# Moving one group's statistics, a few evictions and the first head sums in the prologue of a gated cross-attention block

## The chip, the cores and the metric

One core of one Trainium2 chip. The metric is the device time of one execution in microseconds (us). Times inside a profile count from the start of its span. All arithmetic is float32.

## The reference, cut to what matters

```python
x = x + tanh(g_xattn) * attention(layernorm(x), ctx)   # 16 heads of 64, softmax over 77 keys, then Wo and bo
x = x + tanh(g_ffn) * (layernorm(x) @ W[idx] + b[idx])  # idx: the arg max of logits + gumbel noise
```

x is (4, 2048, 512), the context (4, 77, 384). The layernorms divide by the standard deviation of each row.

## The kernel before, in words

The 8192 rows of x are cut into 16 groups of 512 rows, four groups per batch entry. Weights are folded first: Wq and the keys become one matrix `m` per batch entry (scores = x @ m), the values and Wo become `vo` (attention output = p @ vo), and the chosen W, centred and scaled by its gate, becomes `wf`. So each group needs three products: scores, attend, and the feed-forward one.

Each product is a `Seven`: a block multiplication done with seven half-size products instead of eight. `product(s)`, for s = 0 to 6, issues the matmuls of one of the seven on TensorE (L461). `post(s)` takes its PSUM bank out: for three or four of the seven it is a copy by ScalarE (L467), for the others an addition by VectorE (L486). Two of the three banks of a `Seven` are read and then added to further: product 2 adds to the bank that `post(0)` has read, product 4 to the one that `post(2)` has read, product 6 to the one that `post(4)` has read. So a late `post` stops TensorE. The extra operands (T1 to T4) are sums made by GpSimd (L432), those of the weights likewise (L123).

The order of the work is written out by hand, and each engine takes its instructions in that order. A PSUM pool has seven banks for matmul results. The change lies in the prologue, which TensorE passes between 53 and 150 us:

1. `s0`, `s1`, `s2` for group 0: scores in three `Seven`s. Between their steps stand the layernorm statistics of groups 0 and 1, and the weights `wf`: `centre_wf` (a matmul with ones at L637, four VectorE subtractions at L639) and `scale_wf` (eight ScalarE activations at L644).
2. `s0` for group 1, and between its steps the last of eight `build_vo(p, engines)`: six matmuls each (L331), six evictions with the gate's scale, by VectorE (L334) or ScalarE (L336) as the letters of `engines` say in turn, and four stores to DRAM by SyncE's queue. Beside it runs the softmax of group 0: `head_max` (L524, L526), 64 exponentials on ScalarE (L532, each 128x77), `head_sum` (L539 and a reciprocal, L540) and `head_scale` (GpSimd, L543).
3. `s1` and `s2` for group 1 together, twelve matmul records a step. Between their steps `p_columns` transposes the softmax result of group 0 on VectorE (L552; each transpose reads all four heads).

Then the loop over groups 1 to 15 starts with `at` for group 0 (tile `ps_a`), then the feed-forward product (`ps_f`) with the first scores of a later group laid between.

The statistics of a group (class `Norms`) have four steps: `stats` (16 VectorE BN statistics, L365), `gather` (eight ScalarE copies, L374), `calc` with `power` (seven small VectorE operations, L381 to L388, and a power on GpSimd, L393), and `back` (four ScalarE copies, L398, then `down` and `up` on GpSimd, L403 and L404). `norm_step(n, 0)` is `gather`, `norm_step(n, 1)` is `calc` and `power`, `norm_step(n, 2)` is `back`. Group 1's `down` and `up` are first read by its `head_max` and exponentials, in the loop.

Of the kernel before, what the change touches and what calls it, by code (L numbers as in the profile page):

```python
# [19 lines left out]
def flamingo_block_kernel(  # L20
# [34 lines left out]
    NT, D = x.shape  # L55
# [32 lines left out]
    def bank(name):  # L88
        return pm.tile([P, 512], F32, tag="mm", name=name)
# [29 lines left out]
    def weight_sum(w, n, engine=None):  # L119

        to, a, b_, op = ((5, 0, 3, ALU.subtract), (3, 3, 2, ALU.add), (4, 3, 0, ALU.subtract),
                         (6, 1, 4, ALU.subtract))[n]
        (engine or nc.gpsimd).tensor_tensor(flat(w[:, to]), flat(w[:, a]), flat(w[:, b_]), op)  # L123
# [23 lines left out]
    xg, ys, ts_ = {}, {}, {}  # L147
# [4 lines left out]
    def load(i):  # L152
        xg[i] = row_tile("xg")
        for a in range(NA):
            nc.sync.dma_start(out=xg[i][ts(a, 32)], in_=rows_of(x, i)[:, :, ts(a, P)])
# [33 lines left out]
    def by_chunk(t):  # L189

        return t.rearrange("p (a q e) -> p q a e", a=NA, e=32)

    def chunked(t):
        return t.rearrange("p (q a e) -> p q a e", a=NA, e=32)
# [127 lines left out]
    def build_vo(p, engines):  # L322
        n = 0
        for c in range(3):
            r = min(P, BP - c * P)
            for hh in range(2):
                stg = vo_st[(2 * p + hh) % len(vo_st)]
                hr = ts(hh, DH)
                v = vT[p][hr].rearrange("p r b k -> p (r b k)")
                ps = bank("ps_vo")  # L330
                nc.tensor.matmul(ps[:r, :], v[:, ds(c * P, r)], wo[hr, p, :], start=True, stop=True)  # L331
                src, dst = by_chunk(ps[:r, :]), chunked(stg[:r, c, :])
                if engines[n % len(engines)] == "D":
                    nc.vector.tensor_scalar(dst, src, tgx[:r], None, ALU.mult)  # L334
                else:
                    nc.scalar.activation(dst, src, AF.Copy, scale=tgx[:r])  # L336
                n += 1
        for hh in range(2):
            d, stg = vo_d[2 * p + hh], vo_st[(2 * p + hh) % len(vo_st)]
            nc.sync.dma_start(out=d[0 : 2 * P].rearrange("(c r) e -> r c e", r=P), in_=stg[:, 0:2])  # L340
            nc.sync.dma_start(out=d[2 * P :], in_=stg[: BP - 2 * P, 2])
# [5 lines left out]
    def load_vo(bi):  # L347
        src = vo_d.rearrange("h (r b k) e -> (h r) b k e", b=B, k=NK)[:, bi]
        for o, c in ((0, 0), (1, 0), (1, 1), (0, 1)):
            nc.sync.dma_start(out=vo[:, BLK[o, c]], in_=src[:, ts(c, KH), ts(o, D // 2)])  # L350
# [161 lines left out]
    def s_rows(i, k, cols):  # L512
        if i not in sc:
            sc[i] = wp.tile([P, HA, NG, JP], F32, tag="s", name="s")
        nc.vector.transpose(key_chunk(sc[i], k), cols.rearrange("p (g h r) -> p g h r", h=HA, r=R))  # L515

    def head(i, h):
        return sc[i][:, h, :, :J]
# [3 lines left out]
    def head_max(i, h):  # L522
        mx = stat[:, ds((16 + h) * NG, NG)]
        nc.vector.tensor_reduce(mx, head(i, h), AX.X, ALU.max)  # L524
        nmx[h] = small.tile([P, NG], F32, tag=f"nmx{h}", name="nmx")
        nc.vector.tensor_tensor(nmx[h], mx, norms[i].down, ALU.mult)  # L526

    def exps(i, n0, n1):

        for n in range(n0, n1):  # L530
            h, g = n // NG, n % NG
            nc.scalar.activation(head(i, h)[:, g, :], head(i, h)[:, g, :], AF.Exp,  # L532
                                 scale=norms[i].up[:, g : g + 1], bias=nmx[h][:, g : g + 1])
# [3 lines left out]
    def head_sum(i, h):  # L537
        sums[h] = sm = small.tile([P, NG], F32, tag=f"sm{h}", name="sm")
        nc.vector.tensor_reduce(sm, head(i, h), AX.X, ALU.add)  # L539
        nc.vector.reciprocal(sm, sm)  # L540

    def head_scale(i, h):
        nc.gpsimd.tensor_tensor(head(i, h), head(i, h), sums[h].unsqueeze(2).to_broadcast([P, NG, J]),  # L543
                                ALU.mult)

    def p_columns(i, k0, k1):
        for k in range(k0, k1):
            if k == 0:
                t = wp.tile([P, NK * T + KH * T2], F32, tag="pT", name="pT")
                pT[i] = Columns(t[:, : NK * T].rearrange("p (n t) -> p n t", t=T),  # L550
                                T1=t[:, NK * T :].rearrange("p (n t) -> p n t", t=T2))
            nc.vector.transpose(pT[i].all[:, k, :].rearrange("p (g h r) -> p g h r", h=HA, r=R),  # L552
                                key_chunk(sc[i], k))
# [75 lines left out]
    def sum_wf(wfr):  # L629
        t = wf_f[:, :D]  # L630
        nc.gpsimd.tensor_tensor(t, wfr[:, 0, :], wfr[:, 1, :], ALU.add)
        nc.gpsimd.tensor_tensor(t, t, wfr[:, 2, :], ALU.add)
        nc.gpsimd.tensor_tensor(t, t, wfr[:, 3, :], ALU.add)

    def centre_wf(wfr):
        ps = bank("ps_w")
        nc.tensor.matmul(ps, ones, wf_f[:, :D], start=True, stop=True)  # L637
        for c in range(NDC):
            nc.vector.tensor_tensor(wfr[:, c, :], wfr[:, c, :], ps, ALU.subtract)  # L639

    def scale_wf(wfr):
        for c in range(NDC):
            for o in range(2):
                nc.scalar.activation(chunked(wf[:, BLK[o, c // 2], c % 2, :]),  # L644
                                     by_chunk(wfr[:, c, :])[:, ts(o, 2)], AF.Copy, scale=tgf)
# [10 lines left out]
    def norm_step(n, s):  # L656
        if s == 0:
            n.gather()
        elif s == 1:
            n.calc()  # L660
            n.power()
        elif s == 2:
            n.back()
# [20 lines left out]
    for s in range(7):  # L684
        s1.product(s)
        if s == 0:
            s1.post(0)
            s0.product(6)
            s0.post(6)
            norm_step(n, 0)  # L690
            for k in range(2):
                s_rows(0, KH + k, s0.chunk(1, k))
            sum_wf(wfr)
        elif s == 1:
            norm_step(n, 1)
        elif s < 4:
            n1.stats(xg[1], 0, 8 * (s - 2), 8)
        if 0 < s:
            s1.post(s)
        if s == 3:  # L700
            norm_step(n, 2)
            norm_step(n1, 0)
        if s == 4:
            centre_wf(wfr)
        if s == 5:
            scale_wf(wfr)
            for k in range(2):
                s_rows(0, 2 + k, s1.chunk(0, k))
# [3 lines left out]
    for s in range(7):  # L712
        s2.product(s)
        s2.post(s)
        if s == 0:
            norm_step(n1, 1)
        if s == 3:
            norm_step(n1, 2)
        if s == 5:
            s_rows(0, 4, s2.chunk(0, 0))  # L720
            load(2)
# [14 lines left out]
    for s in range(6):  # L736
        s0.product(s)
        s0.post(s)
        if s < 4:
            build_vo(4 + s, "D" if s == 2 else "DDA")  # L740
        if s < 2:
            head_max(0, 2 + s)
        exps(0, e[s], e[s + 1])
        if s == 3:
            load_vo(0)
        if s in (2, 4, 5):
            h = (None, None, 0, None, 1, 2)[s]
            head_sum(0, h)
            head_scale(0, h)
    for s in range(7):  # L750
        s1.product(s)
        s2.product(s)
        if s == 0:
            s1.post(0)
            s2.post(0)
            exps(0, 57, 64)
            s0.product(6)
            s0.post(6)
            weight_sum(wf, 0)
            head_sum(0, 3)  # L760
            head_scale(0, 3)
        if 1 <= s < 5:
            p_columns(0, (0, 2, 5, 7)[s - 1], (2, 5, 7, 10)[s - 1])
        if s == 2:
            pT[0].sum("T1")
        if s == 3:
            weight_sum(vo, 0)
        if s == 4:
            weight_sum(vo, 1)
        if s == 5:  # L770
            weight_sum(vo, 2)
            for k in range(4):
                s_rows(1, (0, 1, KH, KH + 1)[k], s0.chunk(k // 2, k % 2))
        if 0 < s:
            s1.post(s)
            s2.post(s)
# [161 lines left out]
    n1, n0 = Norms(NGRP + 1, NG // 2), Norms(NGRP + 2, NG // 2)  # L938
# [144 lines left out]
```

## Time and profile before

| | |
|---|---|
| three timed runs | 1263.45, 1261.90, 1262.99 us; median 1262.99 |
| the profiled execution | 1262.86 us, its span 1261.1 us |
| busy: TensorE matmul, weight load | 1241.8 us, 1060.5 us |
| busy: VectorE, ScalarE, GpSimd | 915.6, 686.3, 876.8 us |
| mean granted TensorE clock | 0.996 |

The span runs from the first to the last instruction; 1.8 us of the execution lie around it. "Busy" is the sum of an engine's instructions. A bracket behind an instruction in a timeline is the time that its engine stood idle before it, and the arrow names what ended that. PEclk is the clock that TensorE was granted, 1.00 being full speed. A name such as `snap L467` is the tile that an instruction writes and its line in the kernel.

### The profile page before, as it was taken

To read this page: it belongs to the slowest core of one execution; us is meant where nothing else is said; L and a number is where in the kernel's file an instruction comes from. 1 tells how busy PE (TensorE), PEld (TensorE's weight loads), DVE (VectorE), ACT (ScalarE), POOL (GpSimd) and SP (SyncE) were. 2 spreads that over 40 slices of the span, in tenths; PEclk is the share of its full clock that TensorE was granted. 3 is DMA by queue.
4 is the path that set the end of the run, shared out by engine and by line. 5 is a ranking of instruction groups with operands and counts; after the bars stand their busy time and mean duration, and the time that the engine had idled before them with its cause. 6 is when DMAs were issued, how large, how long until landed. Compare 5 with 4: busy or idle time off the path is not lost.

```text
span 1261.1 us, 16981 instructions
## 1 busy us (share of the span) xinstructions
PE 1241.8 (98%) x5704; PEld 1060.5 (84%) x5704; DVE 915.6 (73%) x1857; ACT 686.3 (54%) x1966; POOL 876.8 (70%) x470
## 2 busy tenths in 40 slices
PE   9999899999999999999999999999999999999996
PEld 6565788888888888888888888888888888888885
DVE  5788766777776767777776777666777876666577
ACT  3447473827456483736548373654738274564823
POOL 4343796685968778584968778575986877585766
PEclk9999999999999999999999999999999999999999
DMA  9776400304106030303306030122304111010102
GB/s 267 275 219 209 117 1 1 68 21 110 20 1 151 1 67 1 66 2 90 62 1 151 1 67 1 24 44 84 67 1 109 43 42 26 1 34 1 34 1 67
DMA packets 95221, 80.27 MB, mean 64 GB/s; under 512 B 3856, under 2 KB 83088, under 8 KB 95136
## 3 DMA queue, kind: packets, MB, share of 16 engines
q1 hardware_dynamic: 92768, 76.74, 24.1%
q10 hardware_dynamic: 1760, 1.34, 0.3%
q8 instruction: 45, 0.74, 0.3%
q0 software_dynamic: 608, 1.13, 0.2%
q14 instruction: 40, 0.33, 0.1%
HBM read 44.07 MB, written 35.13 MB: 63 GB/s over the span
## 4 chain that ended last, share of the span: by engine, by line
PE 94%; DVE 3%; ACT 2%; POOL 0%; issue 0%; DVEq 0%; POOLq 0%; ACTq 0%
PE ps_a L461 38%; PE ps_s L461 36%; PE ps_f L461 15%; PE ps_kv L266 2%; PE ps_vo L331 1%; PE ps_m L296 1%; ACT s L532 1%; DVE pT L552 0%; PE ps_w L167 0%; DVE vo L334 0%; DVE snap L486 0%; ACT wf L644 0%; ACT snap L467 0%; DVE t L412 0%; DVE z L219 0%
## 5 line engine op out<-in xcount | busy, mean ns | idle before, releaser
L461 PE MATMUL ps_a<-pT,vo 128*128 128x256 f32 x2240 | 486.2, 379 | 0.0
L461 PEld LDWEIGHTS ps_a<-pT,vo 128*128 128x128 f32 x2240 | 425.6, 190 | 57.9
L532 ACT ACTIVATE s<-s,nmx,up 128x77 f32<-128x77 f32 x1024 | 355.8, 444 | 0.0
L432 POOL TENSOR_TENSOR pT<-pT 128x1280 f32<-128x1280 f32 x64 | 185.8, 2904 | 173.2 <-PE ps_a L461 163.7
L461 PE MATMUL ps_s<-tq,m 128*128 128x256 f32 x1280 | 293.0, 381 | 6.0 <-DVE sn L486 3.3
L461 PEld LDWEIGHTS ps_s<-tq,m 128*128 128x128 f32 x1280 | 243.4, 191 | 44.1 <-DVE sn L486 3.7
L467 ACT COPY snap<-ps_s 128x512 f32<-128x512 f32 (+1 forms) x188 | 93.5, 515 | 283.5 <-DVE t L412 131.3
L461 PE MATMUL ps_s<-xc,m 128*128 128x256 f32 x960 | 221.4, 380 | 0.0
L461 PEld LDWEIGHTS ps_s<-xc,m 128*128 128x128 f32 x960 | 182.0, 190 | 29.0 <-DVE vo L334 2.4
L543 POOL TENSOR_TENSOR s<-s,sm 128x1232 f32<-128x1232 f32 x64 | 145.2, 2269 | 65.2 <-DVE sm L540 50.2
L486 DVE TENSOR_TENSOR snap<-snap,ps_s 128x512 f32<-128x512 f32 (+1 forms) x141 | 83.4, 593 | 122.7 <-PE ps_s L461 118.6
L461 PE MATMUL ps_f<-tq,wf 128*128 128x256 f32 x512 | 118.4, 379 | 0.4 <-DVE snap L486 0.4
L552 DVE STREAM_TRANSPOSE pT<-s 128x512 f32<-128x512 f32 x160 | 101.0, 677 | 15.9 <-POOL s L543 15.9
L393 POOL TENSOR_TENSOR r<-r,neghalf 32x16 f32<-32x16 f32 (+1 forms) x33 | 93.1, 2832 | 25.8 <-DVE r L388 25.2
L539 DVE TENSOR_REDUCE sm<-s 128x16 f32<-128x1232 f32 x64 | 91.5, 1430 | 25.8 <-ACT s L532 25.8
L432 POOL TENSOR_TENSOR tq<-xc,tq 128x512 f32<-128x512 f32 x64 | 85.3, 1332 | 34.8 <-PE ps_f L461 32.3
L461 PEld LDWEIGHTS ps_f<-tq,wf 128*128 128x128 f32 x512 | 97.2, 190 | 13.9 <-issue 0.7
L515 DVE STREAM_TRANSPOSE s<-snap 128x512 f32<-128x512 f32 x156 | 99.8, 685 | 8.6 <-ACT snap L467 6.4
L524 DVE TENSOR_REDUCE ps_st<-s 128x16 f32<-128x1232 f32 x64 | 92.4, 1444 | 2.1
L432 POOL TENSOR_TENSOR tq<-xc 128x512 f32<-128x512 f32 x64 | 81.6, 1274 | 14.4 <-DVE xc L407 13.1
L461 PE MATMUL ps_f<-xc,wf 128*128 128x256 f32 x384 | 90.7, 379 | 0.0
L467 ACT COPY snap<-ps_f 128x512 f32<-128x512 f32 x63 | 36.9, 586 | 89.1 <-PE ps_f L461 89.1
(126 smaller groups left out, 1183.6 us busy)
## 6 DMA issues: line engine op xcount, KB each, us to landing
xg<-in_x_dram SPq DMA_DIRECT2D x64, 256.0 KB, 6.0
out_dram<-y SPq DMA_DIRECT2D x60, 256.0 KB, 4.5
vo<-vo_d SPq DMA_DIRECT2D x16, 640.0 KB, 6.7
vo_d<-vo SPq DMA_DIRECT2D x16, 512.0 KB, 4.2
m<-m_d SPq DMA_DIRECT2D x12, 640.0 KB, 4.2
m_d<-vo SPq DMA_DIRECT2D x4, 960.0 KB, 7.5
wq<-in_WqT_dram SPq DMA_DIRECT2D x8, 256.0 KB, 6.3
wq<-in_Wo_dram SPq DMA_DIRECT2D x1, 2048.0 KB, 13.8
```

The source lines that it names most:

```text
L266: nc.tensor.matmul(ps[:, :n], w[:, c, ts(p, P)], keys[:, c].rearrange("p b j -> p (b j)"), start=(c == 0), stop=(c == NCC - 1))
L393: nc.gpsimd.tensor_tensor(r, r, neghalf[:32, : r.shape[1]], ALU.pow)
L432: (engine or nc.gpsimd).tensor_tensor(self.at[name], self.at[a], self.at[b_], op)
L461: nc.tensor.matmul(self.ps[r][:, n, :], self.w(blk, c, pair), self.cols(cname, c), start=(first and n == 0 and c == 0), stop=(c == h - 1), ...
L467: nc.scalar.copy(dst, self.ps[r])
L486: nc.vector.tensor_tensor(c, c, self.ps[r], ALU.add)
L515: nc.vector.transpose(key_chunk(sc[i], k), cols.rearrange("p (g h r) -> p g h r", h=HA, r=R))
L524: nc.vector.tensor_reduce(mx, head(i, h), AX.X, ALU.max)
L532: nc.scalar.activation(head(i, h)[:, g, :], head(i, h)[:, g, :], AF.Exp, scale=norms[i].up[:, g : g + 1], bias=nmx[h][:, g : g + 1])
L539: nc.vector.tensor_reduce(sm, head(i, h), AX.X, ALU.add)
L543: nc.gpsimd.tensor_tensor(head(i, h), head(i, h), sums[h].unsqueeze(2).to_broadcast([P, NG, J]), ALU.mult)
L552: nc.vector.transpose(pT[i].all[:, k, :].rearrange("p (g h r) -> p g h r", h=HA, r=R), key_chunk(sc[i], k))
```

## The change

In words, in the order of the program:

- Group 1's 16 BN statistics stand in four lots of four, in steps 2 to 5 of group 0's `s1` and each behind that step's `post`, instead of two lots of eight ahead of the `post`s of steps 2 and 3. Its `gather` stands in step 5 (ahead of `scale_wf`) instead of step 3.
- Its `calc` and `power` stand in step 2 of `s2` instead of step 0, its `back` in step 3 of the later loop of group 1's `s1` and `s2`, instead of step 3 of group 0's `s2`.
- Of `build_vo(7)`, two of the six evictions (one of 128x512, one of 64x512) go from ScalarE to VectorE. `build_vo(6)` was by VectorE alone before as well.
- Head sums and scales 0, 1, 2 of group 0 stand in steps 3, 4, 5 of group 1's `s0` instead of steps 2, 4, 5.
- The last seven exponentials stand ahead of the loop of `s1` and `s2`, so ahead of the copies of its first step.

```diff
@@ group 0, s1
         elif s == 1:
             norm_step(n, 1)
-        elif s < 4:
-            n1.stats(xg[1], 0, 8 * (s - 2), 8)
         if 0 < s:
             s1.post(s)
+        if 2 <= s < 6:
+            n1.stats(xg[1], 0, 4 * (s - 2), 4)
         if s == 3:
             norm_step(n, 2)
+        if s == 5:
             norm_step(n1, 0)
         if s == 4:
             centre_wf(wfr)
@@ group 0, s2
         s2.post(s)
-        if s == 0:
+        if s == 2:
             norm_step(n1, 1)
-        if s == 3:
-            norm_step(n1, 2)
@@ group 1, s0
         if s < 4:
-            build_vo(4 + s, "D" if s == 2 else "DDA")
+            build_vo(4 + s, "DDA" if s < 2 else "D")
...
-        if s in (2, 4, 5):
-            h = (None, None, 0, None, 1, 2)[s]
-            head_sum(0, h)
-            head_scale(0, h)
+        if 3 <= s:
+            head_sum(0, s - 3)
+            head_scale(0, s - 3)
+    exps(0, 57, 64)
@@ group 1, s1 and s2
             s1.post(0)
             s2.post(0)
-            exps(0, 57, 64)
             s0.product(6)
...
+        if s == 3:
+            norm_step(n1, 2)
```

No instruction is added or removed; those named change their place, and two change their engine.

## The prediction

> **What bounds the kernel now.** I read the page's busy times first, then TensorE's waits in the prologue, the granted clock around the longest of them, and the chain that ended last.
>
> ```profile
> PE 1241.8 (98%) x5704; PEld 1060.5 (84%) x5704; DVE 915.6 (73%) x1857; ACT 686.3 (54%) x1966; POOL 876.8 (70%) x470
> ```
>
> TensorE is busy 98% of the span, and from 149.81 us to the last groups it shows no idle time. An edit in the prologue is therefore worth what it changes in TensorE's stops before that. These are the stops between 50 and 152 us (in all, times, longest):
>
> ```profile
> PE ps_s L461 <- DVE sn L486: 3.3, 1, 3.3
> PE ps_s L461 <- ACT snap L467: 1.8, 2, 1.5
> PE ps_s L461 <- DVE vo L334: 0.8, 1, 0.8
> PE ps_vo L331 <- DVE snap L486: 0.5, 1, 0.5
> ```
>
> The longest has a tail, which the busy time and granted clock of two stretches show (PEclk is the third figure from the end):
>
> ```profile
> 142.00:145.40 3.40, 0.12 (x1) 0.00 (x0) 3.40 (x8) 0.00 (x0) 3.40 (x2) 1.00 0.01 2
> 145.40:149.80 4.40, 4.37 (x12) 3.53 (x13) 4.40 (x9) 0.59 (x1) 4.26 (x2) 0.61 0.00 0
> ```
>
> Behind the stop the clock averages 0.61, and the twelve matmul records of product 6 take 4.54 us where the twelve before took 2.75. So this stop, E, costs 3.31 + 1.79 = 5.1 us. The 1.46 us stop at 91.69, called B, left the clock at 1.00.
>
> What makes E: the chain that ended last runs there
>
> ```profile
> 131.22 2.42 ACT s L532 x7
> 133.63 0.02 issue
> 133.66 1.45 DVE sm L539
> 135.10 0.02 issue
> 135.13 0.26 DVE sm L540
> 135.39 0.02 issue
> 135.42 0.02 POOLq L543
> 135.43 0.09 issue
> 135.53 2.28 POOL s L543
> 137.80 0.02 issue
> 137.82 0.91 DVE pT L552 x2
> ```
>
> The last exponentials, the last sum and the last scale come ahead of every transpose; post(4), which frees product 6, stands behind ten transposes. What makes B is on ScalarE, here with VectorE's row for the statistics:
>
> ```profile
> 82.09 3.18 DVE L365 BATCH_NORM_STATS2 s<-xg 128x6 f32<-128x128 f32 x16
> ...
> 87.59 3.30 ACT L644 ACTIVATE wf<-wfr,tg 128x256 f32<-128x256 f32 x8
> ...
> 90.80 1.10 ACT L467 COPY snap<-ps_s 128x512 f32<-128x512 f32 x3
> ...
> 91.69 1.13 PE L461 MATMUL ps_s<-tq,m 128*128 128x256 f32 x4 [1.46 <-ACT snap L467]
> ```
>
> TensorE waits for the second of three copies behind scale_wf. Ahead of scale_wf stand the eight gather copies, 85.97 to 87.58.
>
> **Part 1: statistics and gather.** The 16 statistics cost the same 3.18 us, but the last four now stand behind post(3), post(4) (1.25 together), the four subtractions of centre_wf (2.46) and post(5) (0.67). From 82.09 VectorE was busy without a gap until 89.44, and it does the same work in another order: the matmuls that it needs end at 82.17, 83.89, 84.75 and 86.48, each in time. So the last statistic ends at 89.5 instead of 85.27. post(4) is 1.5 us earlier; that lets product 6 of s1 start at 86.32 instead of 86.50, which only lengthens a stop that follows anyway.
>
> gather needs the last statistic, so ScalarE waits from 86.1 to 89.5, and behind the waiting copy are queued gather's other seven (1.61 in all, to 91.1), scale_wf (3.30, to 94.45) and the copies that TensorE waits for. The second of these let TensorE go 0.80 behind scale_wf's end. TensorE resumes at 95.26: B grows by 3.57, from 1.46 to 5.0 us.
>
> Is the clock reduced there? The rows show 1.46 us without and 3.31 us with a reduction. 5.0 lies beyond the second, so I take a reduction, at E's price of 1.79 us. The bounds: 0, and 3.6, twice E's, if the spell is twice as long.
>
> The Trainium skill, "TensorE: Matmul & The Clock Gate" (section "What's actually happening"), says that a free-running window of 3413 ns in which TensorE idles halves its clock. Read strictly, 5.0 us hold a whole window in (5.0 - 3.41) / 3.41 = 47% of the positions; as an estimate that prices the reduction at 0.47 x 1.7 = 0.8 us and the sum below at -1.4. The trace disagrees in part: 3.31 us, less than a window, were enough.
>
> **Part 2: calc and back.** calc stays behind the transposes that wait for s1's last copy, as in the trace (92.63, behind a transpose that waited for ScalarE); it goes along with the 3.57. back leaves a bad place: ScalarE waited 4.32 us for the power and did four copies (0.84) ahead of s2's post(6), which ended at 98.78. Without them post(6) follows product 6 at once: with TensorE 3.57 later it ends at 100.35, only 1.6 later, and group 0's first maximum with it. In its new place back takes 0.85 on ScalarE, inside an idle stretch of 13.50 us; if that cover were gone it would cost 0.85. Its down and up (0.48) stand on GpSimd between T1 and the sums of vo, and that counts below.
>
> **Part 3: evictions, sums, exponentials.** From here all times are at full clock. TensorE starts build_vo(3) at 96.30 + 3.57 = 99.87. It took 24.83 to product 4 of s0 (121.13). In that lie the stops of 0.82 and 0.55, and bank waits inside build_vo(5) (3.20 instead of 2.92) and build_vo(7) (4.18 less 0.55, instead of 3.0). VectorE is now less behind TensorE, so the freed banks come in time: 24.83 - 0.82 - 0.55 - 0.28 - 0.63 = 22.55, product 4 at 122.4.
>
> VectorE: a first eviction follows its matmuls' start by 1.16 (69.73 to 70.89). build_vo(6) starts at 114.5, so its six evictions run from 115.6 for 4.03, to 119.7; post(3) to 120.3; build_vo(7) starts at 119.4, its six evictions run from 120.6 to 124.6. Two of them are new here (0.68 each). Then head_sum 0, 1.42 + 0.25 with gaps, to 126.3; it was at 118.88.
>
> ScalarE: exponentials 24 to 31 end at about 119.9 and nothing stands between them and the rest. In the trace 4.64 us lay between (117.19 to 121.83: two evictions of 0.69 and 0.68, two waits of 1.77 and 1.59, gaps). The other 32 take 32 x 0.346 = 11.1, so the last ends at 131.0 instead of 133.66. That is 2.7 earlier, but late next is GpSimd: scale 0 starts at 126.45, each scale takes 2.27 and a gap, and wf's sum (1.27) stands ahead of the fourth. 126.45 + 4 x 2.28 + 1.27 = 136.85, against 137.80.
>
> From the first transpose to TensorE's restart were 7.61 us (137.82 to 145.43): now 136.87 to 144.5. TensorE arrives at 122.4 + 20.99 = 143.4, the same work as from 121.13 to 142.12. E is 1.1 us, less than B's 1.46, which left the clock alone. Product 6 takes 2.6, and ps_a starts at 147.1 instead of 149.81: -2.7.
>
> **Part 4: what GpSimd gives back.** From 154.37 GpSimd works without a gap past the feed-forward's first sum, and that sum is just in time:
>
> ```profile
> 154.37 5.78 POOL L432 TENSOR_TENSOR pT<-pT 128x1280 f32<-128x1280 f32 x2 [1.64 <-PE ps_a L461]
> ...
> 180.25 1.27 POOL L432 TENSOR_TENSOR tq<-xc 128x512 f32<-128x512 f32 x1
> ```
>
> It ends at 181.52, and TensorE takes it at 181.75. In the changed kernel T1 follows the transposes by 3.17 (140.04), takes 2.91, then down and up 0.48, then three sums of vo 8.87: 152.3. TensorE's first attend product ended before that (151.4). So this run starts 2.07 earlier, not 2.7, and the feed-forward sum ends at 179.45, where TensorE would be at 179.05. The gain shrinks to 2.07 plus the slack of 0.2, about 2.2 us.
>
> The vo stores on SyncE's queue follow the last eviction, 2.6 us later than before, and vo's loads follow these. They landed within 10.6 us of issue; issued from about 128.9 they are in by 141.5, before the sums need them at 143.4. No cost; if they were later, GpSimd would wait one for one.
>
> **Sum.** -2.2 at full clock, +1.79 for the reduction behind B, which shifts all later steps alike: -0.4. The profiled execution took 1262.86, so **1262.5 us**. The runs' median, 1262.99, lies 0.13 above it.
>
> **Rivals.**
> 1. The clock stays full behind B: -2.2, 1260.7 us. For it: no row has a stop of 5 us. Against it: 3.31 sufficed. 16%.
> 2. The spell behind B lasts twice as long: +3.6 instead of +1.8, 1264.3 us. For it: it rests on one spell only. 12%.
> 3. Slower: E stays long as well and its clock reduction comes back. The place is the row of twelve VectorE evictions, head sum 0 and four GpSimd scales. If they end 2.3 us later than summed, E is over 3.3 again, and the total is -0.4 + 2.3 + 1.8 = +3.7: 1266.6 us. For it: head sum 0 stands 7.4 us later than in the trace, behind all evictions; one eviction by itself lasts 0.74, and they waited 0.67 at 113.22. Against it: 12 x 0.07 + 0.67 makes 1.5, not 2.3. 14%.
> 4. gather isn't held up, and B stays 1.46: another 3.57 and no reduction, 1257.1 us. Against it: the copy is ahead of scale_wf in ScalarE's order, and needs the last statistic. 5%.
> 5. The edit does not reach E: the gain at E and the loss at B cancel, 1262.9 us. 5%.
>
> The forecast has the remaining 48%.
>
> **The numbers.** 0.2%, about 2.5 us, is what a measurement of this kernel can tell from no change. Faster by more (under 1260.5): rival 4, a good third of rival 1 (its time lies 0.2 above the bound, and my sums are good to about 0.8), and 6% from the forecast's edge: 17%. Slower by more (over 1265.5): most of rival 3 (13%) and 2% of rival 2: 15%. Within: 68%. The range leaves out rival 4 and rival 3's larger part and holds the clock's bounds (0 to 3.6) with 0.8 of error: 1259.9 to 1265.4.
>
> **What would show it.** Right: the first L374 copy of group 1 idles about 3.4 us for VectorE's L365; TensorE stops some 5 us for snap L467 near 95, with PEclk below 1 behind it; E is near 1 us with PEclk 1.00 behind it; the four scales run nearly back to back; TensorE waits briefly for tq L432 near 180. Wrong: a B under 3 us, an E over 3, or a new stop after 150 us of more than 1.

## The result, and the profile after

| | before | changed |
|---|---|---|
| median of 12 runs each | 1263.40 us | 1262.35 us |
| lowest, highest | 1261.90, 1263.85 | 1260.29, 1263.31 |
| profiled execution, its span | 1262.86, 1261.1 | 1261.98, 1260.2 |

The ratio is 0.9994, with a 95% interval of 0.9986 to 1.0002: no difference that these runs can tell. Beneath it two large ones cancel. These are TensorE's waits between 50 and 200 us in the changed kernel (in all, times, longest), to be read against the four lines of before:

```profile
PE ps_s L461 <- ACT snap L467: 5.6, 2, 5.3
PE ps_s L461 <- DVE sn L486: 0.8, 1, 0.8
PE ps_f L461 <- POOL tq L432: 0.3, 1, 0.3
```

E has shrunk from 3.3 to 0.8 us, and the stops of 0.8 and 0.5 us at the evictions are gone. B has grown from 1.5 to 5.3 us. A new short stop waits for GpSimd's feed-forward sum. How B came about, in the timeline of ScalarE and TensorE (start, duration, in brackets the idle time before):

```profile
89.07 0.19 ACT L374 COPY ps_st<-s 32x32 f32<-32x32 f32 x1 [3.46 <-DVE s L365]
...
90.69 3.30 ACT L644 ACTIVATE wf<-wfr,tg 128x256 f32<-128x256 f32 x8
93.90 1.10 ACT L467 COPY snap<-ps_s 128x512 f32<-128x512 f32 x3
...
94.78 2.07 PE L461 MATMUL ps_s<-tq,m 128*128 128x256 f32 x4 [5.30 <-ACT snap L467]
```

The first gather copy idles 3.46 us for the last statistics. The same eight activations of 3.30 us and the same copies follow, and TensorE goes on after the second of these. The four matmul records there take 2.07 us; before, they took 1.13. The clock tells why (stretches; the first figure behind the length is TensorE's busy time, the third from the end the granted clock):

```profile
88.80:92.10 3.30, 0.68 (x4) 0.25 (x2) 1.39 (x3) 2.93 (x12) 0.00 (x0) 1.00 0.00 0
92.20:95.50 3.30, 0.72 (x2) 0.63 (x3) 1.01 (x2) 2.79 (x8) 0.00 (x0) 0.50 0.00 0
95.60:98.90 3.30, 3.30 (x9) 2.58 (x9) 2.07 (x9) 0.37 (x1) 1.21 (x1) 0.50 0.00 0
99.00:102.00 3.00, 3.00 (x15) 2.13 (x16) 1.78 (x5) 0.37 (x1) 2.92 (x3) 1.00 0.00 0
```

The clock is halved from 92.16 to 98.99 in the trace's clock record, 2.6 us of it inside the stop and 4.2 behind it. From the restart to build_vo(3) TensorE takes 6.57 us (94.78 to 101.35) instead of 4.61 (91.69 to 96.30): the reduction costs 1.96 us.

E, in the timeline of GpSimd, VectorE and TensorE:

```profile
127.85 6.72 POOL L543 TENSOR_TENSOR s<-s,sm 128x1232 f32<-128x1232 f32 x3 [22.20 <-issue]
134.52 1.26 POOL L123 TENSOR_TENSOR wf<-wf 128x512 f32<-128x512 f32 x1
135.75 2.27 POOL L543 TENSOR_TENSOR s<-s,sm 128x1232 f32<-128x1232 f32 x1
...
138.05 4.27 DVE L552 STREAM_TRANSPOSE pT<-s 128x512 f32<-128x512 f32 x7 [4.17 <-POOL s L543]
...
145.65 2.86 PE L461 MATMUL ps_s<-tq,m 128*128 128x256 f32 x12 [0.81 <-DVE sn L486]
```

The last exponentials end at 132.1 and the last reciprocal at 133.9, but GpSimd works through the row of scales without a gap until 138.0. In the profile before, GpSimd stood idle for 2.73 us ahead of the last scale, waiting for the last sum and so for the last exponentials; now its own row of scales sets when the transposes start. The twelve records behind E take 2.86 us, where they took 4.54.

One reading to be careful with: the chain that ended last names a DMA of `xg` (135.38 to 144.08) as what released `down` at 144.08. `down` reads nothing of `xg`; it stands behind T1 on GpSimd, which ran from 141.21 to 144.1. The two ends coincide.

### The profile page after: what moved, and what is told of

Its sections match the earlier page's. It is cut to its first block, busy times and chain, and to the rows that moved or that the text cites. A ratio compares the mean times of both kernels' runs of the same rounds, so it can differ in the third digit from the quotient of the medians.

```text
span 1260.2 us, 16984 instructions
## 1 busy us (share of the span) xinstructions
PE 1241.3 (99%) x5704; PEld 1061.0 (84%) x5704; DVE 914.0 (73%) x1859; ACT 685.6 (54%) x1964; POOL 876.8 (70%) x470
## 3 DMA queue, kind: packets, MB, share of 16 engines
q0 software_dynamic: 608, 1.13, 0.4%
## 4 chain that ended last, share of the span: by engine, by line
PE 93%; POOL 3%; DVE 2%; ACT 1%; DMA 1%; issue 0%; SPq 0%; POOLq 0%; DVEq 0%; ACTq 0%
PE ps_s L461 36%; PE ps_a L461 36%; PE ps_f L461 15%; PE ps_kv L266 2%; PE ps_vo L331 2%; PE ps_m L296 2%; POOL vo L123 1%; DMA xg<-in_x_dram 1%; POOL pT L432 1%; PE ps_w L167 0%; POOL s L543 0%; DVE snap L486 0%; POOL xc L558 0%; ACT wf L644 0%; POOL wf L123 0%
```

## Experiments

The theory was that of the prediction. B: gather's wait delays scale_wf, the copies and TensorE, and the longer stop halves the clock. E: the row of evictions, exponentials, sums, scales and transposes is shorter, until GpSimd bounds it. The ratios are to the kernel before, run on the same chip.

**e1: gather moved behind the copies**

```diff
@@ changed kernel, group 0's s1
-        if s == 5:
-            norm_step(n1, 0)
@@ s2, behind post(s)
+        if s == 1:
+            norm_step(n1, 0)
         if s == 2:
             norm_step(n1, 1)
```

> The changed kernel with group 1's gather moved behind post(1) of s2, so that scale_wf is not behind the last statistic. Theory (the gather's wait is what makes stop B long, and the reduced clock follows from it): TensorE's wait for snap L467 near 90 falls from 5.3 to under 1.5 us, the granted clock there stays 1.00, and the run is 4.5 + 1.9 = 6.4 us faster than the changed kernel, near 1256. Rival (the statistics laid between the posts hold VectorE up, whatever gather does): B stays near 5 and the time near 1262. Rival (everything before E is absorbed at E by something that does not move, such as the loads of vo): B falls, E grows by as much, time near 1262.

Measured: 1256.13 us, ratio 0.9948 (0.9934 to 0.9962) to before. TensorE's waits:

```profile
PE ps_s L461 <- ACT snap L467: 0.8, 2, 0.5
PE ps_s L461 <- DVE sn L486: 0.8, 1, 0.8
```

The statistics are as spread as in the change. The clock stays full, B is down to 0.5, and E is the same 0.8. So the price in the changed kernel was that of gather's place alone, about 6 us (ratios 0.9994 and 0.9948), and nothing later absorbs it.

**e2: statistics and gather as before, the rest as changed**

```diff
@@ changed kernel, group 0's s1
+        elif s < 4:
+            n1.stats(xg[1], 0, 8 * (s - 2), 8)
         if 0 < s:
             s1.post(s)
-        if 2 <= s < 6:
-            n1.stats(xg[1], 0, 4 * (s - 2), 4)
         if s == 3:
             norm_step(n, 2)
-        if s == 5:
             norm_step(n1, 0)
```

> The changed kernel with the statistics and the gather of group 1 where they stood before the change; evictions, head sums, exponentials and the late return stay. Theory: B is back at 1.5 us and full clock, E stays near 0.8, time near 1262.35 - 3.6 - 1.9 = 1257. Rival (the spread statistics are part of what shortens E): E returns to 3 us and its reduced clock, time near 1263.

Measured: 1257.07 us, 0.9954 (0.994 to 0.9967). B is 1.47 us at full clock and E 0.81:

```profile
PE ps_s L461 <- ACT snap L467: 1.8, 2, 1.5
PE ps_s L461 <- DVE sn L486: 0.8, 1, 0.8
```

The spread of the statistics has no part in E's gain; the rest of the change is worth 5.7 us by itself (1262.78 to 1257.07).

**e3: the statistics and the gather alone.** The edit of e2 turned round, made in the kernel before.

> The kernel before with only the statistics and the gather moved as in the change. Theory: B grows to 5 us with a reduced clock behind it and E stays at 3.3 us with its own, so the time is that of before plus 3.6 + 1.8 = 5.4 us, near 1268.8. Rival (a longer B is absorbed in E): at most 2 us slower, near 1265.

Measured: 1267.10 us, 1.0035 (1.0022 to 1.0049): 4.4 us slower (2.8 to 6.2), an interval that holds the 5.4 expected, with the median a microsecond below it. B is 5.30, E 3.31, and the clock falls behind both. The profile shows the missing microsecond: from build_vo(3) to the end of E TensorE takes 48.02 us (102.19 to 150.21) instead of 49.13 (96.30 to 145.43), mostly because the 0.82 us stop of before is not there any more. My expectation had left that out. The reduction behind B costs 1.55 us here: from the restart to build_vo(3) are 6.16 us (96.03 to 102.19) instead of 4.61. The windows at B are of use further below:

```profile
89.20:92.50 3.30, 1.52 (x8) 0.99 (x6) 2.23 (x7) 2.08 (x10) 0.00 (x0) 1.00 0.00 0
92.60:95.90 3.30, 0.00 (x0) 0.00 (x0) 0.16 (x1) 3.30 (x10) 0.00 (x0) 1.00 0.00 0
96.00:99.30 3.30, 3.27 (x8) 2.65 (x9) 2.69 (x9) 0.61 (x2) 0.36 (x1) 0.50 0.00 0
```

**e4: the stop filled with matmuls**

```diff
@@ changed kernel, group 0's s2
         s2.product(s)
+        if s == 1:
+            fill = bank("ps_w")
+            for c in range(4):
+                nc.tensor.matmul(fill, ones, xc[0].all[:, c, :], start=True, stop=True)
         s2.post(s)
```

> The changed kernel with four extra matmuls of 128x512 (about 3.5 us, into a bank that nothing reads) behind product 1 of s2, so that TensorE works through most of stop B. Theory (the reduced clock behind B costs 1.9 us of its own): granted clock 1.00 behind B, the stop itself falls to about 1.8 us because the extra matmuls lie in it, product 2 still starts at the same time, and the run is 1.9 us faster than the changed kernel, near 1260.4. Rival (the slower products are hidden, since ScalarE and VectorE are late there anyway): clock 1.00 but the time stays near 1262.3.

Measured: 1260.19 us, 0.9981 (0.9972 to 0.999). The extra matmuls took 3.60 us, the stop left is 1.87, product 2 starts at 95.03, and the clock is full around it:

```profile
89.57 3.60 PE L718 MATMUL ps_w<-xc,ones 128*128 128x512 f32 x8
95.03 1.13 PE L461 MATMUL ps_s<-tq,m 128*128 128x256 f32 x4 [1.87 <-ACT snap L467]
```

```profile
89.00:93.00 4.00, 4.00 (x12) 1.82 (x10) 1.44 (x4) 3.58 (x14) 0.00 (x0) 1.00 0.00 0
93.00:96.00 3.00, 1.13 (x6) 0.87 (x5) 1.25 (x3) 2.25 (x7) 0.00 (x0) 1.00 0.00 0
```

From product 2 to build_vo(3) TensorE takes 4.62 us (95.03 to 99.65), 1.95 less than the changed kernel's 6.57, and E is 0.81 as there. Work that nobody needs makes the kernel faster: by 2.2 us between the medians, by 1.6 between the ratios, whose intervals overlap a little. The 1.95 us in the trace are the price of the halved clock, and the run's time shows that they are not hidden.

**e5, e6, e7: the three edits at E, each alone in the kernel before**

```diff
@@ e5: the return
-        if s == 0:
+        if s == 2:
             norm_step(n1, 1)
-        if s == 3:
-            norm_step(n1, 2)
...
+        if s == 3:
+            norm_step(n1, 2)
@@ e6: the evictions
-            build_vo(4 + s, "D" if s == 2 else "DDA")
+            build_vo(4 + s, "DDA" if s < 2 else "D")
@@ e7: head sums and last exponentials
-        if s in (2, 4, 5):
-            h = (None, None, 0, None, 1, 2)[s]
-            head_sum(0, h)
-            head_scale(0, h)
+        if 3 <= s:
+            head_sum(0, s - 3)
+            head_scale(0, s - 3)
+    exps(0, 57, 64)
...
-            exps(0, 57, 64)
```

> The kernel before with only calc, power and back of group 1 moved as in the change. Theory (E is a row of engines in turn, and each of the three edits there shortens it by its own wait): ScalarE no longer waits 4.3 us ahead of post(6) of s2, so the exponentials run some 2 us earlier; the 0.82 us stop near 105 goes; E falls to about 2 us and its clock reduction with it; near 1260.5, 2.5 us faster than before. Rival (back's move does nothing, since ScalarE waits again at the evictions of build_vo(7)): E 3.3 us with its reduced clock, time within 1 us of before.

> The kernel before with only the two evictions of build_vo(7) moved from ScalarE to VectorE. Theory: 25 exponentials start near 117.2 instead of 121.8, the last ends near 131, the first transpose starts near 135 instead of 137.8, E falls under 1 us with full clock; near 1258.7, 4.4 us faster. Rival (each of the three edits gives a third of what all give together): 2 us faster, near 1261. Rival (VectorE, with 1.4 us more of evictions, becomes late): no gain.

> The kernel before with only the head sums in steps 3, 4, 5 and the last seven exponentials ahead of the loop. Theory: post(3) and build_vo(7)'s evictions no longer stand behind head sum 0 on VectorE, so the 0.55 us stop near 119 goes and ScalarE's evictions end 1.7 us earlier; the last exponential ends near 131.2; E falls to about 1.5 us with full clock; near 1259, 4 us faster. Rival (each edit gives a third): 2 us faster. Rival (the sums, later by 3 to 5 us, make GpSimd's scales late): no gain.

| | us | ratio to before | E | clock behind E |
|---|---|---|---|---|
| before | 1263.03 | | 3.31 | halved |
| e5, return | 1261.35 | 0.9989 (0.998 to 0.9998) | 3.32 | halved |
| e6, evictions | 1258.68 | 0.9966 (0.9954 to 0.9978) | none | full |
| e7, sums, exponentials | 1259.66 | 0.9974 (0.9964 to 0.9983) | 0.66 | full |

e6 met its expectation. e7 came within 0.7 us of its own, with a smaller E than I expected and a new stop that I had not foreseen:

```profile
PE ps_s L461 <- ACT sn L467: 1.6, 1, 1.6
```

The copies of the first s1 and s2 step stand behind the last exponentials there, and product 2 needs them. The changed kernel and e2 have no such stop: there ScalarE has no evictions of build_vo(7), for which it still waits 1.79 and 0.37 us in e7, so the exponentials end earlier against TensorE. For e5 my expectation was wrong, and its rival had E right:

```profile
144.41 4.20 PE L461 MATMUL ps_s<-tq,m 128*128 128x256 f32 x12 [3.32 <-DVE sn L486]
```

The 0.82 us stop is gone, but E is untouched. TensorE reaches the feed-forward product 1.02 us earlier than before (179.01 and 180.03), little more than that stop. ScalarE still waits 1.73 and 1.59 us for its evictions in build_vo(7). One of those matmuls stops TensorE for 0.55 us for post(3), which waits on VectorE behind head sum 0. TensorE and the chain behind E meet at that matmul, so whatever is won ahead of it moves both alike.

The three gains, measured between the medians, are 1.7, 4.4 and 3.4: 9.4 together, and 5.7 in e2, where all three stand. E with its clock can be won only once.

**e8: GpSimd's order (made in e1's kernel)**

```diff
+            head_sum(0, 3)
+            head_scale(0, 3)
             weight_sum(wf, 0)
-            head_sum(0, 3)
-            head_scale(0, 3)
-        if s == 3:
+        if s == 1:
             norm_step(n1, 2)
```

> The kernel of e1_gather_late with two more moves on GpSimd: the sum for wf behind the fourth scale instead of ahead of it, and back in step 1 instead of 3, so that down and up lie ahead of T1, where GpSimd waits for the transposes. Theory (GpSimd's row of scales is what ends E in the changed kernel, and its row from T1 to the feed-forward's first sum what stops TensorE near 180): E's 0.81 us and the 0.23 us stop for tq L432 both go, near 1255.1, about 1 us faster than e1_gather_late. Rival (the last exponential or VectorE's transposes end E): E stays at 0.8.

Measured: 1255.18 us, 0.9939 (0.9925 to 0.9953). TensorE's waits between 50 and 200 us, all of them:

```profile
PE ps_s L461 <- ACT snap L467: 0.8, 2, 0.5
PE ps_s L461 <- DVE snap L486: 0.3, 1, 0.3
```

GpSimd's four scales now follow one another without a gap, with the sum for wf behind them:

```profile
122.79 8.95 POOL L543 TENSOR_TENSOR s<-s,sm 128x1232 f32<-128x1232 f32 x4 [20.21 <-issue]
131.70 1.26 POOL L123 TENSOR_TENSOR wf<-wf 128x512 f32<-128x512 f32 x1
```

E and the stop at the feed-forward sum are both gone, so GpSimd's order made both. The profiles show the gain over e1 as 0.81 + 0.23 us of stops; the medians differ by 0.95, and their runs overlap. The median of e8 is the lowest of all versions.

## Why the prediction was right, point by point

The forecast was 1262.5 us; the median is 1262.35, inside the range. The mechanism holds, and the sizes to about 0.4 us. That the two times agree to 0.15 us is partly luck: the forecast took 0.4 off a profiled execution of 1262.86, while the twelve runs of before have their median at 1263.40, 1.05 above that of the changed kernel. Between the two profiled executions lie 0.88 us, but not all of it is the change. In the profile after, TensorE is already 0.45 us earlier than in the profile before when it reaches product 2 of s1 (78.00 and 78.45): the first matmuls took longer and a stop of 0.68 at 46 us is missing, both far ahead of the first moved instruction. What is left is -0.43, against -0.4 predicted: -2.39 at full clock (-2.2 predicted) and +1.96 for the reduction (+1.79). In the table the 0.45 is taken off the summed times.

| step | predicted | measured |
|---|---|---|
| idle of the first gather copy | 3.4 | 3.46 |
| B; TensorE resumes | 5.0; 94.8 | 5.30; 94.78 |
| clock reduction behind B | +1.79 | +1.96, and 1.95 against e4; 1.55 in e3 |
| product 4 of s0 starts, with that reduction | 123.7 | 123.86 |
| last exponential ends | 132.3 | 132.1 |
| first scale on GpSimd | 127.8 | 127.85 |
| first transpose | 138.2 | 138.05 |
| E, clock behind it | 1.1, full | 0.81, full |
| stop at the feed-forward sum | about 0.4 | 0.26 |

- **Part 1, gather's wait.** Right, and e1 and e2 show it from both sides. The doubtful piece was the clock: I took a reduction because 5.0 lies beyond E's 3.31, at E's price. e4 measures it apart. That the size came out near is partly luck. E's price was read 0.1 too high, since 1.79 compares 4.54 us with 2.75, while twelve records behind a stop take 2.86 at full clock (the changed kernel): it was 1.68. And the price varies with where the halved spell falls: with the same stop of 5.30 us, e3 paid 1.55 and the changed kernel 1.96.
- **Part 2, the return.** post(6) of s2 ends 0.48 us behind the start of build_vo(3), as summed (101.83 and 101.35). In e5, post(6) ends 1.9 us earlier than before (96.86 and 98.78), but the exponentials start only 1.0 earlier (101.40 and 102.40), because ScalarE then waits 0.68 us for build_vo(3); and none of that lead reaches E there.
- **Part 3, late next is GpSimd.** Right: the exponentials end 1.5 us before their old time (133.66 to 132.1) although B is 3.8 us longer, and the row of scales runs on for 4 us behind the last reciprocal. e8 moves 1.27 us out of that row and E goes.
- **Part 4, what GpSimd gives back.** Right in place and size: TensorE stops 0.26 us for the sum, until 180.71; gone in e8.
- **Rivals.** 1 and 2 (clock full, or twice as long) did not happen in the profile. Two of the twelve runs took 1260.29 and 1260.57, near rival 1's time. Their mean granted clock was 0.995, as in six of the other ten runs; the runs of e1, e2, e4, e6, e7 and e8, whose profiles show no reduction, have 0.997 or 0.998. So these two had a reduction as well; how long it was, and why they were 2 us faster, stays open. Rival 3's place was the right one to watch, but each six evictions of build_vo(6) and build_vo(7) took 4.03 as summed, with waits of 0.67 and 0.26 ahead of them. Rival 4 did not happen, as gather waited 3.46 us; e2, with B at 1.47 us, shows that its price of 1257.1 was right (1257.07). Rival 5 gives the same total as the truth, and the profile refutes it: E was reached, and paid for at B.

## What to carry to other kernels

A time that doesn't move can be two changes of 6 us each: read the stops of the bounding engine one by one, and test the parts apart. Before a producer is moved later, look at the first instruction that waits for it and at what is queued behind that on its engine. Price a stop with the clock behind it: here stops of up to 1.9 us cost only themselves (1.87 in e4, at full clock), and those over 3 us cost 1.5 to 2 us more.

## What the runs showed of the hardware

The clock was halved in windows of 3.41 us whose place differs from run to run. In the traces' clock records the halved spells last 3.41 us (145.63 to 149.04 in before, 145.76 to 149.17 in e5, 95.99 to 99.40 and 150.60 to 154.01 in e3) or twice that (92.16 to 98.99 in the changed kernel), and the full clock between the two spells of e3 lasts 51.20 us, fifteen times 3.41. In before the spell began 0.20 us behind TensorE's restart, in the changed kernel 2.62 us ahead of it. In e5 the stop of 3.32 us lay across a boundary:

```profile
142.40:145.70 3.30, 1.29 (x6) 1.16 (x7) 3.30 (x7) 0.00 (x0) 3.30 (x4) 1.00 0.00 0
145.80:149.10 3.30, 3.30 (x9) 2.63 (x8) 3.30 (x7) 0.96 (x2) 3.22 (x2) 0.50 0.00 0
```

TensorE was busy for 1.29 of 3.30 us (39%) in the first window, and yet the clock fell for the whole of the next, in which TensorE never stopped. In e3 a window with 1.52 of 3.30 (46%) left the clock at 1.00. So in these runs the border lies between 39% and 46% of busy time, not at an idle window. The other windows agree: those with 0 and 11% (e3), 6% (before), 22 and 23% (the changed kernel) were followed by a halved one, those with 55% (e7), 57% (e2) and 61% (e6) by a full one. Whether it is the share of busy time that counts, or the length of the idle piece in the window (2.01 us in e5, 1.78 in e3), these runs don't tell. In the changed kernel a window with 0.72 of 3.30 (22%) kept the clock down, and a full one released it. The Trainium skill, "TensorE: Matmul & The Clock Gate" (section "What's actually happening"), speaks of at least one idle window; here a window that was 39% busy was enough, which fits the profile of before, where a stop of 3.31 us, less than a window, halved the clock.
